# A four-layer spectral network with a dilation behind it: a new order of fc1 and fc2 steps in the mixing, and loads moved away from the rows of layers 1 and 3

## The chip, the cores and the metric

The kernel runs on one core of one Trainium2 chip. The metric is the device time of a run in microseconds, and the median over several runs is quoted. One execution was recorded by the hardware profiler; the profile describes that execution alone, and its span is the time from its first to its last instruction.

## What is computed

Eight images of 8 channels and 256 x 256 pixels, fp32 throughout. Cut to what matters:

```python
h = _gconv1x1(concat(groupnorm(x), grid), fc0_w, fc0_b)      # 4 groups, 10 channels each
for i in range(4):
    h1 = _spectral_conv(h, sp_w1[i], sp_w2[i])               # rfft2, 24 x 12 modes mixed, irfft2
    h2 = _gconv1x1(h, w_w[i], w_b[i])
    h = h1 + h2
    if i < 3:
        h = _gswish(h, betas[i])
h = _gswish(_gconv1x1(h, fc1_w, fc1_b), betas[3])            # 10 -> 128 channels in each group
x = x + _gconv1x1(h, fc2_w, fc2_b)                           # 128 -> 2 channels in each group
x = x + dilate3x3(groupnorm(x))                              # maximum over 3 x 3, border -2
```

The Fourier transforms are matrix products with tables of sines and cosines, since only 24 x 12 modes are kept.

## The kernel before

The images run one after another. For image b the kernel goes through four layers, and among their instructions it deals the steps of the "head" (fc1, swish and fc2) of the image before, so that the head's products on TensorE and its Silu on ScalarE fill the time around the layers' VectorE work. A third strand, the "tail" (the dilation), follows the head. Image 0 has no head or tail beside it; the head of image 7 runs alone after the last layer.

The order is written out by hand. Inside the block under a manual schedule the engines TensorE, VectorE, ScalarE and SP (the queue that issues most DMAs) run their instructions in the order in which the Python code emits them. The layers are generators; at each `yield` they hand out a string of letters, and the main loop emits one step for each letter (function `step`, lines 839 to 853):

- `f` first emits the additions to y that are due (`sum_up`), then one fc1 step. `F` is the same without `sum_up`.
- `c` emits one fc2 step and right after it the addition that this step makes due. `C` is the same, with the addition left for a later `f` or `c`.
- `t` emits one step of the tail.

One fc1 step (`first`, line 743) takes 512 pixels: four products on TensorE (line 753), one for each group, into four PSUM banks, and two Silu instructions on ScalarE, one for the first bank (line 754, 512 elements a partition) and one for the other three (line 755, 1536). The result lies in one of four buffers of the tile `act`. One fc2 step (`second`, line 758) uses up two such buffers: eight products (line 770) sum into one bank, and VectorE adds this bank to the tile y (line 777 for the first addition into a y tile, 779 for the others). A head has 128 fc1 and 64 fc2 steps.

PSUM is divided into two tags. `one` is a single bank, with 2 buffers; `tri` is three banks, with 2 buffers. An fc1 step takes one of each, an fc2 step one `one`, and the layers' own products take from the same two tags. A step whose buffer is still to be read by another engine waits for that engine.

The states that fc1 reads lie in DRAM (`stored`, written in layer 3 of the image at line 560). `load_state` (line 724) brings them back into SBUF in pieces of 256 KB (tile `hs`, 4 buffers, line 729), each nine fc1 steps before it is read. `load_y` (line 731) brings 256 KB of the input for the final addition (line 740). Both are issued from SP at the place where the step that calls them is emitted.

Within a layer after layer 0 the stages are:

1. `spectrum_h`: transposes on VectorE (line 359) and products for the Fourier transform over rows (`p_b`, lines 368 and 379). It hands out six `f` and three `c`.
2. `mix` (line 389): twelve VectorE instructions, six products (line 398) and six sums (line 401) in turn, then six short ones and 64 small products on TensorE (`p_f`, line 429, "the fold" below). Its yields in the layers 1 to 3 are the place of the first edit. `n` counts the twelve instructions.
3. `rows_of` (line 449): products that lay the mixed modes out over rows (`p_g`). In layers 0 and 2 these are 10 large products (line 462). In layers 1 and 3 they are 160 small ones (line 468: 32 x 32 weights, 66 columns). VectorE copies the results into `zt` (line 208).
4. `layer`: for each of the 11 chunks of the image the inverse transform and the 1 x 1 convolution (`burst`, `p_z`), and, in layers 0 to 2, the next forward transform.

In layer 3 a generator named `side` (`start` of the next image) is moved on beside the rows and the bursts: twice in the rows and twice in each chunk. It starts with the three loads of mixing weights for layer 0 of the next image (`load_sw`, 400 KB each, line 387), then normalises the next image in 20 steps (`spectrum_x`) and mixes layer 0 of it (`mix` with l == 0, where the weights are read). The weights of the layers 1 to 3 are loaded at the end of the layer before. The two loads of the next image itself (`load_x`, 1 MB each) are issued in the mixing of layer 3, at n == 2. The lines that the first edit touches:

```python
            if l == 0:
                if n % 2 or n > 7:
                    yield
            elif n not in (0, 2, 6, 10):
                yield "CF" if n in (1, 4, 7, 9) else "f"
...
        yield "fc"
```

Of the kernel before, what the change touches and what calls it, by code (L numbers as in the profile page):

```python
# [38 lines left out]
PIX = 2 * HW  # L39
# [6 lines left out]
def fno_dilate_kernel(ctx: ExitStack, tc: tile.TileContext, a: dict, out: bass.AP):  # L46
# [338 lines left out]
    def load_sw(l, k):  # L385
        t = sb.tile([128, G, 2 * WID, WID], F32, tag="sw", bufs=3)
        nc.sync.dma_start(t.rearrange("p g m i -> p (g m i)"), a["spw"][l, k])
        return t

    def mix(b, l, out_):  # L390

        s = [sb.tile([128, 3, 2, WID, G], F32, tag=f"S{i}", bufs=1, name=f"S{i}_{b}_{l}") for i in range(2)]
        bt, sw = out_["bt"], out_["sw"]
        for n in range(12):
            k, k2 = n // 4, n // 2 % 2
            pr = turned[:, 2, 1024 * k2 : 1024 * k2 + 800].rearrange("p (g m i) -> p g m i", g=G, i=WID)
            if n % 2 == 0:
                nc.vector.tensor_tensor(  # L398
                    pr, sw[k], bt[:, k2, k].unsqueeze(2).to_broadcast([128, G, 2 * WID, WID]), ALU.mult)
            else:  # L400
                nc.vector.tensor_reduce(  # L401
                    s[k2][:, k].rearrange("p s o g -> p (s o) g"),
                    pr.rearrange("p g m i -> p m g i"), AX.X, ALU.add,
                )
            if l == 0:
                if n % 2 or n > 7:
                    yield
            elif n not in (0, 2, 6, 10):
                yield "CF" if n in (1, 4, 7, 9) else "f"
            if n == 2 and l == 3 and b + 1 < n_img:  # L410
                load_x(b + 1)
        for i, (x, y, op) in enumerate((
                (s[0][:, :, 0], s[1][:, :, 1], ALU.subtract), (s[0][:, :, 1], s[1][:, :, 0], ALU.add),
                (s[1][:, :, 1], s[0][:, :, 0], ALU.subtract))):
            three = [t[:, :, :9].rearrange("p k (r o) g -> p k r (o g)", r=3) for t in (x, y)]
            nc.vector.tensor_tensor(fs[:, 0:3, i].rearrange("p r k o g -> p k r (o g)"), *three, op)
            nc.vector.tensor_tensor(fs[:, 3, i, :, 0], x[:, :, 9], y[:, :, 9], op)
        yield "fc"

        n_f = 6 * NO * G  # L420
        if l > 0:
            nc.vector.tensor_copy(fz[:, :, :, 24], cz[:, l])
        if l < 2:
            nc.vector.tensor_copy(fz[:, :, :, 25], cz[:, 4 if l == 0 else 3])
        one, tri, banks = ps_four(f"p_f_{b}_{l}")
        for term in range(2):
            for r in range(4):
                for q in range(4):
                    mm(banks[q][part(r), :n_f], fold[part(q), term, :],
                       fs[part(q), r, term : term + 2].rearrange("p t k o g -> p (t k o g)"),  # L430
                       start=term == 0, stop=term == 1)
        if l == 0:
            mr = out_["mr"]
            nc.vector.tensor_tensor(dc[:, 0:1], mr[:, 0:1], mr[:, 1:2], ALU.mult)
            out_["wcn"] = sb.tile([128, 32], F32, tag="wcn", bufs=1, name=f"wcn_{b}")
            nc.vector.tensor_scalar(out_["wcn"], wc, mr[:, 1:2], None, ALU.mult)
            for r in range(4):
                mm(one[part(r), n_f : n_f + NO * G], dc, wm[:, NO * r : NO * (r + 1), :], start=True, stop=True)
        cols = fz.rearrange("p o g c -> p (o g) c")
        nc.vector.tensor_copy(  # L440
            cols[:, :, 6:24].rearrange("p x (q c) -> p q c x", q=3),
            tri[:, :, :n_f].rearrange("p q (c x) -> p q c x", c=6))
        nc.vector.tensor_copy(
            cols[:, :, 0:6].rearrange("p x c -> p c x"), one[:, :n_f].rearrange("p (c x) -> p c x", c=6))
        if l == 0:
            nc.vector.tensor_tensor(
                fz[:, :, :, 24], one[:, n_f : n_f + NO * G].rearrange("p (o g) -> p o g", o=NO), cz[:, 0], ALU.add)

    def rows_of(b, l, side):

        zv = zt[:, :, :, : NBLK * WID].rearrange("p r f (n o) -> p o n r f", n=NBLK)
        yield "ffc"
        for oi in range(NO):
            name = f"p_g_{b}_{l}_{oi}"
            if oi == 0:
                one, tri, banks = ps_four(name)
            else:
                tri = ps_tri(name)
                banks = [tri[:, r, :] for r in range(3)]
            if l % 2 == 0:  # L460
                for r, p in enumerate(banks):
                    mm(p[:, : NBLK * CS * NQ], fz[part(r), oi].rearrange("p g k -> p (g k)"),
                       rowg[part(r)].rearrange("p n j r -> p (n j r)"), start=True, stop=True)
            else:
                for g in range(G):
                    for j in range(NQ):
                        for r, p in enumerate(banks):
                            mm(p[part(j), NBLK * CS * g : NBLK * CS * (g + 1)], fz[part(r), oi, g, :],  # L468
                               rowg[part(r), :, j, :], start=True, stop=True)
            n = NBLK * CS * NQ  # L470
            for i, r in enumerate((1, 2, 3, 0) if oi == 0 else (0, 1, 2)):
                src = banks[r][:, :n]
                if l % 2 == 0:
                    dst = zv[:, NO * r + oi].rearrange("p n r f -> p n f r")
                    src = src.rearrange("p (n f r) -> p n f r", n=NBLK, r=CS)
                else:
                    dst = zv[:, NO * r + oi].rearrange("p n r f -> p f n r")
                    src = src.rearrange("p (f n r) -> p f n r", f=NQ, n=NBLK)
                copy(i, dst, src)
            yield "fcf"[oi]  # L480
            if l == 3 and oi != 1:
                next(side, None)
        if l < 3:
            yield "t"

# [3 lines left out]
            for g in range(G):  # L489
                nc.sync.dma_start(h[32 * g : 32 * g + 6, c].rearrange("p f w -> p (f w)"), a["xp"][b, c, g])  # L490

    def layer(b, l, out_, stored, side):
        group_in_f = l % 2 == 1

        def turn(c, halves=(0, 1)):
# [70 lines left out]
        if l == 3:  # L566
            for c in range(NCH):
                burst(c)
                yield "fct" if c < 8 else "fc"
                next(side, None)  # L570
                if c + 1 < NCH:
                    yield "f"
                next(side, None)
                if c in ((3, 4, 5) if alone[0] else (6, 8, 9)):
                    yield "ready"
                if c > 3 and not alone[0]:
                    read_x(b + 1, c - 4)
            return
# [49 lines left out]

    def start(b, out_):
        if b < n_img:  # L630
            out_["sw"] = [load_sw(0, k) for k in range(3)]
            yield from spectrum_x(b, out_)
            yield from mix(b, 0, out_)

# [8 lines left out]
        for i in range(c, NCH):  # L643
            read_x(b + 1, i)

    def layers(b, stored, d, then):

        for l in range(4):
            if l > 0:
                yield from spectrum_h(b, l, d)
                yield from mix(b, l, d)
            yield from rows_of(b, l, then)
            yield from layer(b, l, d, stored, then)
        yield "stored"
        yield from rest(b, then)

# [47 lines left out]
        yield  # L707


    sums_due = []  # L710

    def sum_up():

        while sums_due:
            sums_due.pop(0)()

    def head(b, stored, stats):
# [6 lines left out]
        def load_state(k):  # L724

            if k < NQ * NCH:
                j, c = k // NCH, k % NCH
                hs[k] = sb.tile([128, PIX], F32, tag="hs", bufs=4, name=f"hs_{b}_{k}")
                nc.sync.dma_start(hs[k], stored[c][:, PIX * j : PIX * (j + 1)])

        def load_y(t):

            if t < 8:
                if last:
                    y = ya[:, 1 + 2 * t : 3 + 2 * t, 1 : HW + 1]
                else:
                    y = sb.tile([128, 512], F32, tag="yp", name=f"y_{b}_{t}")
                    y = y.rearrange("p (s w) -> p s w", s=2)
                box[t] = y
                nc.sync.dma_start(  # L740
                    y, a["x"][b].rearrange("c (p t s w) -> (c p) t s w", p=16, t=8, s=2)[:, t])

        def first():

# [94 lines left out]
    def step(kind):  # L839

        for i, (b, (done, first, second, _)) in enumerate(heads):
            if kind in "fF" and done[0] < STEPS:
                if kind == "f":
                    sum_up()
                return first()
            if kind in "cC" and 2 * done[1] < STEPS:
                second()
# [12 lines left out]
    with tc.manual_schedule(engines={PE, DVE, ACT, SP}):  # L860
# [2 lines left out]
            pass  # L863
        for b in range(n_img):
            stored = [dram.tile([128, NQ * PIX], F32, tag=f"hs{c}", name=f"stored_{b}_{c}") for c in range(NCH)]
            ahead, new, n_ready = {}, None, 0
            for n in layers(b, stored, d, start(b + 1, ahead)):
                if n == "ready":
                    if new is None:
                        if b + 1 < n_img:  # L870
# [9 lines left out]
                else:  # L880
                    for kind in n or "":
                        if kind == "t":
                            tail()
                        elif heads:
                            step(kind)
            d = ahead
        while heads:
            for kind in "ffc":
                if heads:
# [168 lines left out]
```

## Time and profile before

| | us |
|---|---|
| median of 3 runs | 3826.1 (3812.43 to 3826.25) |
| profiled execution, its own time | 3819.83 |
| its span | 3818.0 |
| mean granted TensorE clock, share of full speed | 0.975 |
| ScalarE, Silu of three banks (L755), 1024 times | 1493.3 busy, 1458 ns each |
| ScalarE, Silu of one bank (L754), 1024 times | 616.3 busy, 602 ns each |
| fc1 products (L753) | 1150.2 busy |
| fc2 products (L770) | 1024.3 busy |

The profile names an instruction by engine, line and tiles (`p_fc<-hs,c_w` is a product of the state and a constant into the tile p_fc). PE is TensorE, PEld its loads of weights, DVE VectorE, ACT ScalarE, POOL GpSimd and SP the queue of SyncE. Every fp32 product appears as two instructions, so an fc1 step is 8 products and an fc2 step 16. In the timeline a line gives the start and the length of one instruction or of a run of like ones, and in brackets the idle time of the engine before it with what ended it. Matmuls are pipelined and their ends are modelled; starts are the safer thing to read.

### The profile page before, as it was taken

The numbers are of one execution on the slowest core, as the hardware profiler recorded it, in microseconds if no ns is written. First come the engines' busy times: TensorE is split into PE (matmuls) and PEld (weight loads), VectorE is DVE, ScalarE is ACT, GpSimd is POOL, SyncE is SP. The second block draws the span as 40 slices with busy tenths as digits, with TensorE's granted clock in tenths as the row PEclk, the third lists the DMA queues.
The fourth block names the chain that finished last, engine by engine and source line by source line (L and its number), as shares of the span: only waits on it lengthen the run. The fifth ranks groups of instructions, "written<-read, shape, count | busy, mean of one in ns | idle before, by whom it ended". The sixth has DMA issues, their size and how long they took to land.

```text
span 3818.0 us, 117724 instructions
## 1 busy us (share of the span) xinstructions
PE 3567.4 (93%) x53432; PEld 1299.9 (34%) x53432; DVE 2422.9 (63%) x3781; ACT 2821.9 (74%) x2919; POOL 117.1 (3%) x202
## 2 busy tenths in 40 slices
PE   5768999999999999999999999999999999999997
PEld 2323333333333333333333333333333333333222
DVE  6776665557775667756776577765777566772443
ACT  2435777777777777787777877777777777778986
POOL 1000000000000000000000000000000000000000
PEclk7878999999999999999999999999999999999998
DMA  3005111432225212362123512144222532225221
GB/s 87 15 31 191 49 45 47 147 113 62 73 84 174 82 57 70 99 193 61 49 67 111 185 56 66 53 150 138 59 73 66 174 91 67 67 67 178 79 86 49
DMA packets 114067, 344.91 MB, mean 90 GB/s; under 512 B 15984, under 2 KB 18480, under 8 KB 98144
## 3 DMA queue, kind: packets, MB, share of 16 engines
q1 hardware_dynamic: 95392, 276.32, 24.0%
q0 software_dynamic: 18176, 61.07, 5.0%
q8 instruction: 420, 6.88, 0.8%
q14 instruction: 79, 0.65, 0.1%
HBM read 213.33 MB, written 123.74 MB: 88 GB/s over the span
## 4 chain that ended last, share of the span: by engine, by line
PE 74%; DVE 14%; ACT 5%; issue 4%; DMA 2%; POOL 0%; ACTq 0%; DVEq 0%; POOLq 0%
PE p_fc L770 21%; PE p_fc L753 20%; PE p_z L551 9%; PE p_z L548 7%; PE p_d L516 7%; PE p_z L545 3%; DVE turned L499 3%; PE p_u L530 3%; DVE S L401 2%; ACT act L755 2%; DVE turned L398 2%; DVE y L779 2%; PE p_g L468 2%; DMA yin<-y_rows 2%; ACT act L754 1%
## 5 line engine op out<-in xcount | busy, mean ns | idle before, releaser
L755 ACT ACTIVATE act<-p_fc 128x1536 f32<-128x1536 f32 x1024 | 1493.3, 1458 | 0.0
L753 PE MATMUL p_fc<-hs,c_w 32*128 32x512 f32 x8192 | 1150.2, 626 | 50.1 <-ACT act L754 19.1
L770 PE MATMUL p_fc<-act,c_w 128*32 128x512 f32 x8192 | 1024.3, 602 | 8.2 <-DVE y L779 6.3
L754 ACT ACTIVATE act<-p_fc 128x512 f32<-128x512 f32 x1024 | 616.3, 602 | 417.7 <-PE p_fc L753 408.4
L499 DVE STREAM_TRANSPOSE turned<-h 128x1024 f32<-128x1024 f32 x528 | 632.3, 1225 | 183.0 <-ACT h L556 182.4
L556 ACT ACTIVATE h<-p_z 128x512 f32<-128x512 f32 (+1 forms) x528 | 512.0, 1021 | 226.5 <-PE p_z L551 226.5
L779 DVE TENSOR_TENSOR y<-p_fc,y 128x512 f32<-128x512 f32 x392 | 267.6, 683 | 589.1 <-PE p_fc L770 586.4
L753 PEld LDWEIGHTS p_fc<-hs,c_w 32*128 32x128 f32 x8192 | 363.3, 184 | 638.9 <-ACT act L754 269.8
L770 PEld LDWEIGHTS p_fc<-act,c_w 128*32 128x32 f32 x8192 | 226.5, 109 | 709.8 <-issue 323.1
L551 PE MATMUL p_z<-c_binv,zt 32*128 32x256 f32 x5632 | 411.7, 406 | 0.0
L548 PE MATMUL p_z<-h,c_wt 32*32 32x512 f32 x8448 | 374.3, 607 | 8.4 <-ACT act L754 4.2
L551 PEld LDWEIGHTS p_z<-c_binv,zt 32*128 32x128 f32 x5632 | 259.6, 187 | 311.6 <-issue 298.4
L516 PE MATMUL p_d<-turned,c_fw 32*32 32x480 f32 (+1 forms) x9216 | 308.3, 540 | 0.7 <-DVE turned L499 0.4
L520 ACT ACTIVATE turned<-p_d 128x1440 f32<-128x1440 f32 x144 | 183.1, 1271 | 90.2 <-PE p_d L516 87.0
L558 ACT ACTIVATE h<-p_z,c_bias 128x512 f32<-128x512 f32 (+1 forms) x176 | 186.6, 1111 | 77.9 <-PE p_z L551 77.8
L208 DVE COPY zt<-p_g 128x264 f32<-128x264 f32 x304 | 155.4, 610 | 70.3 <-PE p_g L468 52.7
L401 DVE TENSOR_REDUCE S<-turned 128x80 f32<-128x800 f32 x192 | 188.9, 984 | 5.9
L398 DVE TENSOR_TENSOR turned<-t,B 128x800 f32<-128x800 f32 x192 | 188.7, 983 | 0.9
L516 PEld LDWEIGHTS p_d<-turned,c_fw 32*32 32x32 f32 x9216 | 127.2, 103 | 165.9 <-issue 65.0
L359 DVE STREAM_TRANSPOSE turned<-zt 128x960 f32<-128x960 f32 x96 | 176.7, 1865 | 2.5
L548 PEld LDWEIGHTS p_z<-h,c_wt 32*32 32x32 f32 x8448 | 94.3, 103 | 188.8 <-DVE y L779 54.1
L530 PE MATMUL p_u<-turned,c_stack 128*32 128x480 f32 (+1 forms) x1152 | 136.7, 543 | 11.5 <-DVE turned L519 6.2
(186 smaller groups left out, 1704.2 us busy)
## 6 DMA issues: line engine op xcount, KB each, us to landing
stored<-h SPq DMA_DIRECT2D x88, 1024.0 KB
hs<-stored SPq DMA_DIRECT2D x352, 256.0 KB
t<-in_spw SPq DMA_DIRECT2D x96, 400.0 KB
yin<-y_rows POOLq DMA_DIRECT2D x56, 512.0 KB, 5.3
h<-in_xp SPq DMA_DIRECT2D x352, 48.0 KB
turned<-in_xw SPq DMA_DIRECT2D x16, 1024.0 KB
y<-in_x SPq DMA_DIRECT2D x56, 256.0 KB
y_rows<-y POOLq DMA_DIRECT2D x56, 256.0 KB, 2.5
```

The costliest lines, as they stand in the source:

```text
L398: nc.vector.tensor_tensor(pr, sw[k], bt[:, k2, k].unsqueeze(2).to_broadcast([128, G, 2 * WID, WID]), ALU.mult)
L401: nc.vector.tensor_reduce(s[k2][:, k].rearrange("p s o g -> p (s o) g"), pr.rearrange("p g m i -> p m g i"), AX.X, ALU.add,)
L499: nc.vector.transpose(dst[:, 2 * i : 2 * i + 2], h[:, c, 2 * i : 2 * i + 2].rearrange("p f (s x) -> p f s x", s=2))
L516: mm(banks[q][part(v % 4), : 240 * n], fw8[part(q), v, :], t[part(q), :, :, v, : NBLK * WID], start=v < 4, stop=v >= 4)
L548: mm(o, wt[part(q), l, g, :], h[part(q), c, f, :], start=True, stop=False)
L551: mm(banks[q][:, HW * s : HW * (s + 1)], zt[part(q), 2 * c + s].rearrange("p f o -> p (f o)"), binv[part(q), :], start=False, stop=s == 1)
L556: nc.scalar.activation(dst, src, AF.Silu)
L753: mm(banks[g], w1[part(g), blk, :], hs[k][part(g), :], start=True, stop=True)
L754: nc.scalar.activation(act[:, 0, :], one, AF.Silu)
L755: nc.scalar.activation(act[:, 1:4, :], tri, AF.Silu)
L770: mm(acc[part(g), :], w2[:, g, 15 - rb - i : 47 - rb - i], act[:, g, :], start=i == 0, stop=i == 1)
L779: nc.vector.tensor_tensor(y, sums, y, ALU.add)
```

## The change

There are four edits.

1. In the mixing of layers 1 to 3 the step of n == 1 hands out "fc" in the place of "CF", and those of n == 4, 7 and 9 hand out "fC". The letter `F` is gone, and `step` no longer knows it.
2. `hold(True)` at the start of `rows_of` in layers 1 and 3 (with `hold(False)` in effect in the others) makes `load_state` and `load_y` put their DMA issues on a list; `hold(False)` at the end of the rows issues what is on the list. The tiles are still allotted where they were.
3. The three loads of mixing weights for the next image's layer 0 move from the start of `side` (in the rows of layer 3) to the chunks 1, 2 and 3 of layer 3, one in each, behind that chunk's write of the state on SP. For image 0 they stay at the start of the kernel.
4. The dictionary that receives them is handed through `layers` and `layer` for this.

```diff
             elif n not in (0, 2, 6, 10):
-                yield "CF" if n in (1, 4, 7, 9) else "f"
+                yield {1: "fc", 4: "fC", 7: "fC", 9: "fC"}.get(n, "f")
...
     def rows_of(b, l, side):

         zv = zt[:, :, :, : NBLK * WID].rearrange("p r f (n o) -> p o n r f", n=NBLK)
+        hold(l % 2 == 1)
         yield "ffc"
...
             if l == 3 and oi != 1:
                 next(side, None)
+        hold(False)
         if l < 3:
             yield "t"
...
                 if c in ((3, 4, 5) if alone[0] else (6, 8, 9)):
                     yield "ready"
+                if 0 < c < 4 and b + 1 < n_img:
+                    ahead.setdefault("sw", []).append(load_sw(0, c - 1))
                 if c > 3 and not alone[0]:
                     read_x(b + 1, c - 4)
...
         if b < n_img:
-            out_["sw"] = [load_sw(0, k) for k in range(3)]
+            if b == 0:
+                out_["sw"] = [load_sw(0, k) for k in range(3)]
             yield from spectrum_x(b, out_)
             yield from mix(b, 0, out_)
...
+    held = [None]
+
+    def now_or_later(f):
+
+        if held[0] is None:
+            f()
+        else:
+            held[0].append(f)
+
+    def hold(on):
+
+        due, held[0] = held[0], [] if on else None
+        for f in due or ():
+            f()
...
-                nc.sync.dma_start(hs[k], stored[c][:, PIX * j : PIX * (j + 1)])
+                now_or_later(lambda: nc.sync.dma_start(hs[k], stored[c][:, PIX * j : PIX * (j + 1)]))
...
-                nc.sync.dma_start(
-                    y, a["x"][b].rearrange("c (p t s w) -> (c p) t s w", p=16, t=8, s=2)[:, t])
+                now_or_later(lambda: nc.sync.dma_start(
+                    y, a["x"][b].rearrange("c (p t s w) -> (c p) t s w", p=16, t=8, s=2)[:, t]))
...
-            if kind in "fF" and done[0] < STEPS:
-                if kind == "f":
-                    sum_up()
+            if kind == "f" and done[0] < STEPS:
+                sum_up()
                 return first()
```

## The prediction

> **What bounds the kernel now.** I read the page first, then the groups of TensorE, then the timeline of one mixing stage, then the sums by stretch for all mixing stages and all odd rows, last the waits around line 468. From the page:
>
> ```profile
> span 3818.0 us, 117724 instructions
> PE 3567.4 (93%) x53432; PEld 1299.9 (34%) x53432; DVE 2422.9 (63%) x3781; ACT 2821.9 (74%) x2919; POOL 117.1 (3%) x202
> PE 74%; DVE 14%; ACT 5%; issue 4%; DMA 2%; POOL 0%; ACTq 0%; DVEq 0%; POOLq 0%
> ```
>
> TensorE is busy for 93% and holds 74% of the chain, yet the chain also runs over VectorE and ScalarE. So the question is where TensorE waits. In the mixing stage (lines 389 to 410) of image 3, layer 1, the timeline (start, us, engine, line) has:
>
> ```profile
> 1361.24 1.14 PE L753 MATMUL p_fc<-hs,c_w 32*128 32x512 f32 x8 [0.73 <-ACT act L754]
> 1361.94 0.68 DVE L779 TENSOR_TENSOR y<-p_fc,y 128x512 f32<-128x512 f32 x1
> 1362.68 1.92 PE L770 MATMUL p_fc<-act,c_w 128*32 128x512 f32 x16 [0.30 <-DVE y L779]
> 1364.54 2.02 PE L753 MATMUL p_fc<-hs,c_w 32*128 32x512 f32 x16
> 1365.69 0.60 ACT L754 ACTIVATE act<-p_fc 128x512 f32<-128x512 f32 x1 [1.33 <-PE p_fc L753]
> 1366.49 2.25 PE L770 MATMUL p_fc<-act,c_w 128*32 128x512 f32 x16
> 1367.52 0.61 ACT L754 ACTIVATE act<-p_fc 128x512 f32<-128x512 f32 x1
> 1368.67 2.01 PE L753 MATMUL p_fc<-hs,c_w 32*128 32x512 f32 x16
> 1370.62 2.27 PE L770 MATMUL p_fc<-act,c_w 128*32 128x512 f32 x16
> ```
>
> An fc2 step (L770, "c" below) starts at 1366.49 and the next at 1370.62: a round of one c and two fc1 steps (L753, "f") takes 4.13 us. A c alone holds TensorE 1.85 us (1362.68 to 1364.53), an f 0.88 (the second of two at 1364.54 starts at 1365.42), so a round has 1.85 + 2 x 0.88 = 3.61 us of work. The other 0.52 us is a loop: c, then f behind it, then ScalarE's read of that f's single bank, and only then the next c, which writes that bank. The slot is told by the times: the read L754 at 1365.69 ends at 1366.29, the c starts at 1366.49. The rounds of c at n = 4, 7, 9 all show it; the first shows the two gaps printed. The sums by stretch say that every such stage is alike (us; busy of PE, PEld, DVE, ACT, POOL; granted clock, DMA share, GB/s):
>
> ```profile
> 448.47:469.76 21.29, 20.05 (x152) 5.34 (x152) 15.83 (x24) 17.30 (x19) 0.55 (x1) 1.00 0.22 57
> 679.72:701.01 21.29, 20.04 (x153) 5.34 (x153) 15.83 (x24) 17.30 (x19) 0.54 (x1) 1.00 0.43 146
> ```
>
> 21.29 us in layer 1 at 57 GB/s and in layer 3 at 146: transfers do not matter in it. There are 21 of these (images 1 to 7, layers 1 to 3). The second place is the rows of layers 1 and 3 (line 468, 160 small products each):
>
> ```profile
> L468 PE MATMUL p_g<-c_rowg,fz 32*32 32x66 f32 x5120 | 70.9, 238 | 34.2 <-issue 23.4 <-DVE zt L208 8.9 <-DVE fz L443 1.6
> 1383.60:1393.20 9.60, 6.94 (x352) 4.20 (x348) 4.96 (x9) 3.09 (x3) 0.00 (x0) 1.00 0.21 58
> 1617.50:1629.00 11.50, 9.87 (x352) 4.85 (x348) 7.07 (x13) 3.12 (x3) 0.00 (x0) 0.70 0.11 28
> 1842.50:1850.10 7.60, 6.97 (x352) 4.30 (x351) 4.99 (x10) 3.10 (x3) 0.00 (x0) 1.00 0.27 73
> ```
>
> Equal work takes 7.6 to 11.5 us, and the idle time is "issue": neither data nor a semaphore was late.
>
> **What the Trainium skill says.** "Runtime: NRT & Kernel Launch", Instruction fetch mechanics: instructions are fetched in blocks of 16 KiB (256 instructions) over a DMA queue of the sequencer's own, and crossing a block is mostly hidden. The page's queue q8 (420 packets, 6.88 MB: 16 KB each; 106864 TensorE instructions / 256 = 417) is that stream. In these rows it is not hidden: 128 loads and 128 products pass in 1.5 us, and the stalls of about 2 us (1390.4, 2304.3) end about 2.3 us after their block's packet starts, though the packet takes 0.93. "DMA: Bandwidth & Descriptors", Issuing engines are not separate DMA queues: all queues share 16 engines, so loads can slow a fetch; packets of q8 take 0.88 to 1.6 us here. "TensorE: Matmul & The Clock Gate", What's actually happening: idle TensorE drops to half clock; 0.70 in the stretch at 1617.5 agrees. "PSUM — Partial Sum Buffer", Specifications: 8 banks of 512 fp32. The tiles "one" (2 x 1) and "tri" (2 x 3) fill all, so no f or c gets a spare bank.
>
> **The change part by part.**
>
> (1) Deal in the mixing, lines 408-409. The counts stay 9 f and 5 c; the order c f f | c f f | c f f | c f f | f c becomes f c f | f c f | f c f | f c f | f c... with adds (L779) as before except the first, now right behind its c. No step is added. Before a c the number of f's ahead goes from 3 to 4 acts, which the 4 act buffers just hold, and the last "fc" of the stage already had 4; a c then reads only acts finished long ago (before, its later weight loads waited for ACT L755, which makes 2.25 of 1.92).
>
> I carry the rows above through the new order, each step starting at the latest of: TensorE free (0.88 after an f, 1.85 after a c); its bank free (ScalarE's L754 starts 1.16 us after an f, or 1.83 after the previous f's, lasts 0.60, and 0.20 later TensorE may write; an add ends 2.68 after its c). Banks are taken in the order in which they come free. Clock 13xx: f1 57.52, c1 58.39, f2 60.24, f3 61.12, c2 62.20 (ScalarE's read of f2), f4 64.05, f5 65.55 (add of c2), c3 66.42, f6 68.27, f7 69.15, c4 70.22, f8 72.07, f9 72.95 (its triple bank until 73.24), c5 74.10, and the fold (L429) 75.95. It was at 1378.88, so 2.93 us are saved. The same rules on the old order give its measured starts (59.37, 61.3, 62.68), so I trust them to some 0.3 us. What is late next: ScalarE, 1.83 per f or 3.66 per round, against TensorE's 3.61. Bounds: TensorE's bare sum is 9 x 0.88 + 5 x 1.85 = 17.17 from 57.52, at most 4.19 saved; if f1 takes the bank that L382 frees at 58.12 and f5 one that costs 0.45, 2.0 is saved. I take 2.93: 21 x 2.93 = 61.5 us, range 42 to 88. VectorE (15.8 of 21.3 us) has cover: after the change its two products and sums per round plus the add come to 2.67 x 0.98 + 0.69 = 3.3 us.
>
> (2) Held loads. In rows of layers 1 and 3 the loads of hs (L729, 256 KB) and y (L740) leave SP after the rows instead of in them: one or two hs each, 14 rows. Same number, later by up to 9 us. A state is loaded 9 f's ahead: of the three loads after 1611.08 (1622.47, 1641.75, 1648.49) the third marks its first reader, 37 us later; held to 1629, 19 us remain. A 256 KB transfer takes 2.5 us (y_rows in the page), so nothing waits; SP has no other work in the rows. Were that cover gone, each late us costs up to 14. The queue's next entries, stored and h, come later.
>
> (3) Mixing weights for the next image, 3 x 400 KB. They leave SP at 1611.45 to 1612.44 now, just before the rows; after, behind the stored writes of chunks 1 to 3 of layer 3. First reader: mix of layer 0, 20 steps of the side generator on, at chunk 9, some 40 us after chunk 3. Chunks 1 to 3 carry 400 KB more per 6.6 us, 60 GB/s on the layer's 209; I take 1.5 us in all for slower dilation loads there (0 to 7: six images by about 1 us).
>
> What (2) and (3) bring to the rows: idle time over the 14 rows is 20.8 us beside the 0.63 us wait for zt; layer 3 takes 10.04 us in the mean, layer 1, with less traffic, 8.82. All of this difference gone is 7 x 1.22 = 8.5 us. But the stalls of layer 1 are as long where a block border falls badly (9.6 and 7.6 at like traffic), so contention is the smaller part: a fetch packet slows by 0.1 to 0.5 us. I take 0.35 x 14 = 5 us; from 0 to 9, and about 8 us either way if block borders shift or a half-clock stretch comes or goes (1617.5: 0.70 for 11.5 us, about 3 us).
>
> Sum on the profiled execution (span 3818.0, its own time 3819.83): 3819.8 - 61.5 - 5 + 1.5 = 3754.8. The median of the three runs, 3826.1, lies 6.3 above it; on that base 3761. I say 3760.
>
> **Rivals.**
> (a) TensorE's bare sum: ScalarE never falls behind, 4.19 a stage, rows fully mended: 3826 - 88 - 9 = 3729. For: VectorE and ScalarE each fit into it; against: ScalarE's 3.66 per round. 0.10.
> (b) Only the first gaps go: banks fall less well, 1.0 a stage, 21 us, and nothing in the rows: 3805. For: a bank's choice decides 0.5 us at a time, and the trace has one odd choice, at 1361.24, where f takes the bank of the f before. Against: the loop c-f-ScalarE-c is cut by the order alone. 0.13.
> (c) Slower: c is given the bank of the f just in front of it. Then it waits for that f's read, 1.96 after it instead of 0.88, in each of 5 rounds: a round is 1.96 + 1.85 + 0.88 = 4.69 against 4.13, 0.56 x 5 x 21 = 59 us, less 5: 3880. It decides from the point where more than half of the c's take that bank. Against: the bank of the f before comes free earlier. 0.08.
> (d) It does not reach the end: the 3 us saved are waited out in the rows for ScalarE. For: f9's read ends 1.05 us after the fold starts (0.69 before). Against: that is 0.36 us, and TensorE is the bound behind it. 3820. 0.04.
>
> **How the numbers follow.** The forecast has 0.65, with 3735 to 3795 its own range (2.0 to 4.0 a stage, rows -10 to +9). (a), (b) and it are faster by over 0.5% (19 us, about what this measurement can tell from none): 0.88. (d) is the same: 0.04. (c) 0.08. The range 3732 to 3800 leaves out (c), (d) and parts of (a) and (b).
>
> **What would show it.** Mixing stages of 18.4 us (17.2 to 19.4), rounds of c of 3.7, no wait of L753 for L754 of 0.73 at their start, L770 at 1.92 throughout; odd rows of 9.0 us in the mean with "issue" still there; no wait for hs. Wrong it is if stages keep 21 us, or if c's wait for L754 right after their f.

## The result, and the profile after

| | before | after |
|---|---|---|
| median of 4 runs, us | 3823.33 (3812.43 to 3826.25) | 3765.4 (3764.59 to 3771.87) |
| ratio, with its 95% interval | | 0.9857 (0.9834 to 0.9881) |
| span of the profiled execution | 3818.0 | 3763.8 |

The change makes the kernel 58 us faster by the medians; the two profiled executions differ by 54.2 us. From the page of the changed kernel:

```profile
span 3763.8 us, 117725 instructions
PE 3536.7 (94%) x53432; PEld 1288.3 (34%) x53432; DVE 2423.2 (64%) x3781; ACT 2824.3 (75%) x2919; POOL 117.3 (3%) x202
PE 72%; DVE 16%; issue 5%; ACT 4%; DMA 2%; POOL 0%; ACTq 0%; DVEq 0%; POOLq 0%
```

The instruction counts of all engines are as before, so what has gone is waiting. Of the 54 us, 31 stand in TensorE's busy time (3567.4 us before), since a step that stops in its middle counts as busy. Line numbers have moved: fc1 is L773 now, its Silus L774 and L775, fc2 L790, its additions L797 and L799, the small products of the rows L469. The sums by stretch of two mixing stages (layers 1 and 3 of image 1), with the columns as before:

```profile
447.63:466.73 19.10, 18.60 (x159) 4.83 (x162) 15.82 (x24) 17.36 (x19) 0.55 (x1) 1.00 0.23 63
673.90:693.00 19.10, 18.60 (x156) 4.82 (x156) 15.82 (x24) 17.36 (x19) 0.54 (x1) 1.00 0.45 162
```

All 21 stages have gone from 21.29 to 19.10 us, with the same work on VectorE (15.8) and ScalarE (17.4). The timeline of the same stage that was shown of before (image 3, layer 1):

```profile
1342.59 1.92 PE L790 MATMUL p_fc<-act,c_w 128*32 128x512 f32 x16
1344.44 1.14 PE L773 MATMUL p_fc<-hs,c_w 32*128 32x512 f32 x8
1345.21 0.68 DVE L799 TENSOR_TENSOR y<-p_fc,y 128x512 f32<-128x512 f32 x1
1345.60 0.60 ACT L774 ACTIVATE act<-p_fc 128x512 f32<-128x512 f32 x1
1345.95 1.14 PE L773 MATMUL p_fc<-hs,c_w 32*128 32x512 f32 x8 [0.37 <-DVE y L799]
1347.02 1.93 PE L790 MATMUL p_fc<-act,c_w 128*32 128x512 f32 x16
1348.88 2.02 PE L773 MATMUL p_fc<-hs,c_w 32*128 32x512 f32 x16
1350.83 1.92 PE L790 MATMUL p_fc<-act,c_w 128*32 128x512 f32 x16
```

The round from the c at 1347.02 to the one at 1350.83 takes 3.81 us where it took 4.13. One new wait is printed: the f at 1345.95 waits for an addition that VectorE begins only at 1345.21, because a sum of the mixing stands in front of it. The group of the small products, over the whole run:

```profile
L469 PE MATMUL p_g<-c_rowg,fz 32*32 32x66 f32 x5120 | 68.7, 236 | 23.5 <-issue 11.8 <-DVE zt L208 9.5 <-DVE fz L443 1.6
```

"issue" has fallen from 23.4 to 11.8 us, and the wait for zt has not changed. Summed over all stages, measured from first product to first product, the two spans differ like this:

| stage | before, us | after, us | difference |
|---|---|---|---|
| mixing of layers 1 to 3, images 1 to 7 (with the end of the Fourier step) | 530.7 | 484.6 | -46.1 |
| rows of layer 1, images 1 to 7 | 70.3 | 68.4 | -2.0 |
| rows of layer 3, images 1 to 7 | 77.3 | 67.2 | -10.1 |
| rows of layers 1 and 3, image 0 | 15.1 | 12.4 | -2.6 |
| all else | 3124.6 | 3131.2 | +6.6 |

### The profile page after: what moved, and what is told of

It reads as the page before. It is cut to its first block, busy times and chain, and to the rows that moved or that the text cites. A ratio compares the mean times of both kernels' runs of the same rounds, so it can differ in the third digit from the quotient of the medians.

```text
span 3763.8 us, 117725 instructions
## 1 busy us (share of the span) xinstructions
PE 3536.7 (94%) x53432; PEld 1288.3 (34%) x53432; DVE 2423.2 (64%) x3781; ACT 2824.3 (75%) x2919; POOL 117.3 (3%) x202
## 4 chain that ended last, share of the span: by engine, by line
PE 72%; DVE 16%; issue 5%; ACT 4%; DMA 2%; POOL 0%; ACTq 0%; DVEq 0%; POOLq 0%
PE p_fc L790 19%; PE p_fc L773 18%; PE p_z L553 9%; PE p_z L550 7%; PE p_d L518 7%; PE p_z L547 3%; DVE y L799 3%; DVE turned L501 3%; PE p_u L532 3%; DVE S L401 3%; DVE turned L398 2%; DMA yin<-y_rows 2%; PE p_g L469 2%; DVE turned L359 1%; PE p_b L368 1%
## 5 line engine op out<-in xcount | busy, mean ns | idle before, releaser
L775 ACT ACTIVATE act<-p_fc 128x1536 f32<-128x1536 f32 x1024 | 1492.2, 1457 | 0.3 <-PE p_fc L773 0.3
L773 PE MATMUL p_fc<-hs,c_w 32*128 32x512 f32 x8192 | 1137.7, 627 | 43.2 <-DVE y L799 20.8
L790 PE MATMUL p_fc<-act,c_w 128*32 128x512 f32 x8192 | 1011.7, 602 | 1.8 <-issue 1.7
L774 ACT ACTIVATE act<-p_fc 128x512 f32<-128x512 f32 x1024 | 615.6, 601 | 361.9 <-PE p_fc L773 350.6
L799 DVE TENSOR_TENSOR y<-p_fc,y 128x512 f32<-128x512 f32 x392 | 267.8, 683 | 536.7 <-PE p_fc L790 536.7
L773 PEld LDWEIGHTS p_fc<-hs,c_w 32*128 32x128 f32 x8192 | 356.9, 183 | 615.8 <-ACT act L774 252.6
L790 PEld LDWEIGHTS p_fc<-act,c_w 128*32 128x32 f32 x8192 | 222.1, 109 | 702.8 <-issue 322.1
L560 ACT ACTIVATE h<-p_z,c_bias 128x512 f32<-128x512 f32 (+1 forms) x176 | 186.7, 1111 | 77.3 <-PE p_z L553 77.1
```

The costliest lines, as they stand in the source:

```text
L773: mm(banks[g], w1[part(g), blk, :], hs[k][part(g), :], start=True, stop=True)
L774: nc.scalar.activation(act[:, 0, :], one, AF.Silu)
L775: nc.scalar.activation(act[:, 1:4, :], tri, AF.Silu)
L790: mm(acc[part(g), :], w2[:, g, 15 - rb - i : 47 - rb - i], act[:, g, :], start=i == 0, stop=i == 1)
L799: nc.vector.tensor_tensor(y, sums, y, ALU.add)
```

## Experiments

Eleven runs follow, the last of them the changed kernel again. In every one I read the time, the length of the 21 mixing stages (equal to 0.02 us within a run, but for one stage in each of the two kernels with spread rows) and the mean length of the odd rows of images 1 to 7, from the first to the last small product: 8.82 us in layer 1 and 10.04 in layer 3 before, 8.61 and 8.45 after.

**The order alone.** Edit 1 on the kernel before:

```diff
-                yield "CF" if n in (1, 4, 7, 9) else "f"
+                yield {1: "fc", 4: "fC", 7: "fC", 9: "fC"}.get(n, "f")
```

> Edit 1 alone on the kernel before. If the mixing stage is worth what the two traces show (21.29 to 19.10 us, 21 stages), this run is 46 us faster than before, about 3777, with mixing stages of 19.1 us and odd rows as before (mean 9.4 us). Rival: part of the gain in the rows comes from the order too (the rows start with other buffers free); then the odd rows fall below 9 us here as well and the run is 52 us or more faster.

Measured: 3775.47 against 3824.89 us, ratio 0.9861 (0.9836 to 0.9887), 49 us, between the 46 expected and the 52 of the rival. Stages of 19.10; rows 8.70 and 9.76 us, 9.23 in the mean and not below 9. The order gives the stage and nothing that stands out in the rows; most of the 58 us is here.

**The loads alone.** Edits 2 to 4 on the kernel before, the order as it was.

> Edits 2 to 4 alone on the kernel before. If the loads slow the instruction fetch in the rows: mixing stages stay 21.29 us, the odd rows fall from 9.4 to about 8.5 us in the mean (layer 3 by 1.4 us, layer 1 by 0.3), and the run is 10 to 13 us faster, less up to 4 us in the chunks of layer 3. Rival: the shorter rows after the change are an accident of where the 256-instruction borders fall; then the rows here are as before within 0.3 us in the mean and the time is the same.

Measured: 3814.07 us, 0.9974 (0.9962 to 0.9986), 11 us faster. Stages 21.29 to 21.30; rows of layer 3 8.40, of layer 1 8.73. What stands out is in the rows of layer 3; layer 1 has moved no more than it does between two traces of the changed kernel (8.61 and 8.51). The two halves add up to 60 us; the whole gave 58, and its interval is 45 to 63.

**Which of the loads: states held alone, weights moved alone.** The first keeps the `hold` and `now_or_later` of the change and leaves the weights in the rows; the second takes `hold(l % 2 == 1)` and `hold(False)` out and keeps

```diff
+                if 0 < c < 4 and b + 1 < n_img:
+                    ahead.setdefault("sw", []).append(load_sw(0, c - 1))
```

> Edit 2 alone (states and y held, mixing weights loaded in the rows of layer 3 as before). If the 1.2 MB of weights is what disturbs the rows of layer 3: its rows stay within 0.5 us of 10.0 and those of layer 1 fall by 0.2 to 0.4, the run 2 to 5 us faster. Rival: the states and y matter as much; then the rows of layer 3 fall by 0.7 us or more and the run is 6 us faster or more.

> Edits 3 and 4 alone (mixing weights of the next image moved to chunks 1 to 3 of layer 3, states and y not held). If the weights' 1.2 MB is what disturbs the rows of layer 3, their mean falls from 10.0 to about 8.7 us here too and the chunks of layer 3 lose up to 0.7 us an image; 4 to 8 us faster. Rival: holding the states is what clears the rows; then the rows of layer 3 stay above 9.5 us and the time is the same within 3 us.

Measured: held alone 3818.86 us, 0.9985 (0.9975 to 0.9995), 6 us faster, rows of layer 3 8.62 and of layer 1 9.41 (one of them 13.09, with half clock in it; the other six 8.79). Weights moved alone 3815.61 us, 0.9973 (0.9958 to 0.9988), 11 us faster (4 to 8 expected), rows of layer 3 8.76 and of layer 1 8.89. Either edit clears the rows of layer 3 by itself. The rival of the first had its numbers, but the reason that it gives, the traffic of states and y, is not it. The SP queue shows why. Its issues around the rows of image 3, layer 3, in the kernel before (these rows run from 1617.5 to 1629.0):

```profile
1611.08 0.32 SPq L729 DMA_DIRECT2D hs<-stored  x1
1611.45 1.37 SPq L387 DMA_DIRECT2D t<-in_spw  x3
...
1622.47 0.33 SPq L729 DMA_DIRECT2D hs<-stored  x1
```

In the changed kernel (rows from 1590.9 to 1598.7):

```profile
1584.46 0.32 SPq L749 DMA_DIRECT2D hs<-stored  x1
1593.50 0.32 SPq L749 DMA_DIRECT2D hs<-stored  x1
```

And with the states held alone (rows from 1623.2 to 1631.7):

```profile
1610.78 1.40 SPq L387 DMA_DIRECT2D t<-in_spw  x3
1616.79 0.33 SPq L746 DMA_DIRECT2D hs<-stored  x1
1625.86 0.33 SPq L746 DMA_DIRECT2D hs<-stored  x1
```

The loads of states are not held at all. They leave 6.4 us before the rows and 2.7 us into them, in the changed kernel as in that with the hold alone; before, they left 6.4 us ahead and 5.0 into rows that were longer. What an SP load waits for is its buffer, which comes free when fc1 has read the state in it: each of the loads shown leaves 0.05 to 0.09 us after the last product of an fc1 step. SP has nothing else to do meanwhile, so a load that the code puts behind the rows still leaves at that moment. What the hold does change is the order on SP: before, the three loads of weights stood behind the load at 1611.08 and came out with it, 6 us before the rows; with the hold they stand in front of it and leave at 1610.78, 12.4 us before the rows (1623.2). Before, packets of 1.5 MB start in the six us ahead of these rows; with the hold it is 0.3 MB. Moving the weights away reaches the same end.

So nearly all of the weights pass ahead of the rows. What they do there the fetch packets of the trace tell (queue q8). The last packet that starts before the rows of layer 3, in us from their start, in the images where the borders of the blocks fall alike (to within 24 instructions of 256):

| | images 1, 3 and 5 | image 7 |
|---|---|---|
| before | -0.4, -0.2, -0.6 | -3.5 |
| order alone | -0.6, -0.7, -0.5 | -3.7 |
| states held alone | -3.7, -3.6, -3.6 | -3.0 |
| weights moved alone | -3.6, -3.4, -3.7 | -3.7 |
| after | -3.7, -3.5, -3.5 | -3.7 |

With the weights in front of them these packets start some 3 us later; they take 0.91 to 1.02 us then and are no shorter without. Image 7 has no next image and so no such weights: in the kernel before, its rows take 8.64 us where those of images 1, 3 and 5 take 10.2, 11.5 (with half clock in it) and 9.7.

**What stalls the rows.** 32 small products more at the start of the kernel, half a block of instructions; nothing else moves:

```diff
+    for _ in range(32):
+        mm(p[0:6, 2, :32], fc0x[part(0), :], wt[part(0), 0, 0, :], start=True, stop=True)
```

> Kernel before with 32 more small products (128 TensorE instructions, half a block of 256) at its very start; nothing else moves. If the stalls in the odd rows are set by where the borders of the instruction blocks fall, the rows of layer 1 change places: images 3, 5 and 7 (9.6 to 9.9 us) become short and images 2, 4 and 6 (7.6 to 8.1) long, with about the same sum. Rival: they are set by the loads that happen to run; then each image keeps its length within 0.4 us.

One run: 3820.51 us, the same as before. Sums by stretch of the rows of layer 1 in images 1 to 4:

```profile
479.30:486.70 7.40, 6.77 (x352) 4.35 (x348) 4.96 (x9) 3.11 (x3) 0.00 (x0) 1.00 0.27 76
929.50:939.30 9.80, 7.17 (x352) 4.34 (x348) 4.98 (x9) 3.15 (x3) 0.00 (x0) 0.96 0.21 57
1387.10:1395.10 8.00, 6.93 (x350) 4.21 (x347) 4.97 (x9) 3.15 (x3) 0.00 (x0) 1.00 0.26 70
1840.50:1850.00 9.50, 7.12 (x352) 4.29 (x348) 5.00 (x10) 3.09 (x3) 0.00 (x0) 0.99 0.21 59
```

Before, images 1 to 7 had 9.0, 7.7, 9.6, 7.6, 9.9, 8.1 and 9.8 us; with the shift 7.4, 9.8, 8.0, 9.5, 7.5, 10.0 and 7.5. Long and short have changed places in all seven, at a sum of 59.7 against 61.8. The length of a row in layer 1 is set by where a block border falls in it. In layer 3 the shift alone takes the mean from 10.04 to 9.28 us, with the loads where they were; so there the border counts beside the weights.

The traces show the border itself. Counting TensorE's records (products and loads of weights) from the start of the run, all 226 stalls of over 0.25 us that are put down to "issue" among the small products, in the 13 traces, come behind the 193rd or 194th record of a group of 256, in the shifted kernel too.

**More traffic.** 2 MB more, DRAM to DRAM, issued from SP at the start of each odd row of images 1 to 7:

```diff
+        if l % 2 and b > 0:
+            for i in range(2):
+                t = dram.tile([128, 2048], F32, tag="more", bufs=2, name=f"more_{b}_{l}_{i}")
+                nc.sync.dma_start(t, a["xw"][b, :, i])
```

> Kernel before with 2 MB more of transfers (DRAM to DRAM, read by nobody) issued from SP at the start of each odd row of images 1 to 7. If transfers slow the instruction fetch: fetch packets in these rows take well over 1.1 us in the mean, and the rows of layer 1 grow by 1 us or more each. Rival: the fetch does not feel other traffic; then the rows of layer 1 keep their mean of 8.8 us within 0.4.

One run: 3862.39 us, rows of 12.19 and 12.30 us in the mean. The whole run's group:

```profile
L472 PE MATMUL p_g<-c_rowg,fz 32*32 32x66 f32 x5120 | 76.4, 254 | 54.6 <-issue 45.6 <-DVE zt L208 7.1 <-DVE fz L443 1.6
```

The rows do feel traffic: "issue" has doubled. The other half of the expectation failed. The fetch packet before each of the 26 stalls still takes 0.88 to 1.3 us (one 1.98), and TensorE still goes on 2.2 to 2.7 us after the packet starts (one 3.2); yet the stalls last up to 4.4 us. So the packet is not slower, it starts later: in six of the 26 stalls 0.3 to 2.1 us after TensorE has run dry, where in the kernel before it always started at least 0.26 us ahead of that. There, 19 stalls of over 0.25 us in these rows ended 2.2 to 2.9 us after the start of a fetch packet, and they came to 18.7 us; after, 11 stalls with the same delay came to 10.0 us.

**Why the order helps.** The kernel before with one f more at n == 1 and one fewer at the end:

```diff
-                yield "CF" if n in (1, 4, 7, 9) else "f"
+                yield {1: "fCF", 4: "CF", 7: "CF", 9: "CF"}.get(n, "f")
...
-        yield "fc"
+        yield "c" if l > 0 else "fc"
```

> Kernel before, with one fc1 step more handed out at n == 1 (fCF) and one fewer at the end of the mixing (c for fc). TensorE's order of steps is then that of the changed kernel; the places of the steps and additions among VectorE's twelve instructions stay as before. If the gain comes from a fc2 step that reads acts one step older (4 ahead in place of 3), no fc2 step takes 2.18 us to the next fc1 step any more, and the stage is 18.9 to 19.7 us, 33 to 50 us faster in all. Rival: the gain comes from where the additions stand on VectorE; then the stage stays above 20.5 us and the run is less than 17 us faster.

Measured: 3793.66 us, 0.9908 (0.9889 to 0.9927), 31 us (33 to 50 expected); stages of 19.83 us, 0.13 outside the expected band. No c takes more than 1.93 us there. One f moved from the end of the stage to its front, with the additions where they were, gives 1.46 of the 2.19 us. By the starts of the weight loads, all 21 stages of a kernel are alike. What a step takes beyond 0.88 us (f behind f), 1.07 (c behind f) and 1.85 (any step behind a c), in us a stage:

| | before | this variant | after |
|---|---|---|---|
| second f and second c, at the start | 1.36 | 1.36 | 0 |
| c's that stop in their middle | 0.68 | 0 | 0 |
| third of three f's, at the end | 1.33 | none | none |
| other waits | 0.05 | 0.38 | 1.02 |

One more c behind an f, for one f less behind an f, adds 0.19 to both new orders. So the older acts are worth 0.68 us. More comes from the end of the stage, which was c f f f c: the third f in a row waited for ScalarE to read a three-bank buffer, the longest single wait of the stage.

```profile
1372.81 2.93 PE L753 MATMUL p_fc<-hs,c_w 32*128 32x512 f32 x18
1374.47 1.44 ACT L755 ACTIVATE act<-p_fc 128x1536 f32<-128x1536 f32 x1
1375.96 0.31 PEld L753 LDWEIGHTS p_fc<-hs,c_w 32*128 32x128 f32 x6 [1.05 <-ACT act L755]
```

No run separates the older acts from the shorter row of f's; that both waits are gone is read from the traces. The places of the additions on VectorE give the other 0.73. The wait at the start is as long in this variant as before, with another cause: the f of n == 3 waits for an addition that stands behind two mixing instructions.

```profile
1352.64 0.68 DVE L779 TENSOR_TENSOR y<-p_fc,y 128x512 f32<-128x512 f32 x1
1353.37 1.14 PE L753 MATMUL p_fc<-hs,c_w 32*128 32x512 f32 x8 [1.10 <-DVE y L779]
```

The changed kernel issues that addition at n == 1, right behind its c, and has no such wait there; its other waits, 0.63 us at the f of n == 7 and 0.39 at that of the end, are for later additions.

**Two tries for more.** First, on the changed kernel, the addition of n == 4 at once and the last f one instruction earlier:

```diff
-            elif n not in (0, 2, 6, 10):
-                yield {1: "fc", 4: "fC", 7: "fC", 9: "fC"}.get(n, "f")
+            elif n not in (0, 2, 6, 11):
+                yield {1: "fc", 4: "fc", 7: "fC", 9: "fC"}.get(n, "f")
```

> Changed kernel with the addition of n == 4 right behind its fc2 step (fc for fC) and the step of n == 11 handed out at n == 10. The two waits left in its mixing stage, for the additions at n == 5 (0.6 us) and n == 11 (0.4 us), should go: stages of 18.1 to 18.5 us in place of 19.10, 13 to 20 us faster than the changed kernel. Rival: VectorE, made to wait for fc2 earlier, comes late for its own sums and the fold waits for it; then the stage is 19.1 us or more.

Measured: 3761.06 us, 0.9827 (0.9808 to 0.9847), stages of 18.66 us, short of the 18.1 to 18.5 expected. Between the fold and the rows 0.19 us of that is given back, so 0.25 us a stage remain, which would be 5 us in all, where 13 to 20 were expected. By the times it can't be told from the changed kernel, whose interval it overlaps.

Second, the six steps of an odd row in the same order, but inside the runs of small products:

```diff
-        yield "ffc"
+        yield "ff" if l % 2 else "ffc"
...
                 for g in range(G):
+                    if g == 2:
+                        yield "ccf"[oi]
...
-            yield "fcf"[oi]
+            yield ("f", None, None)[oi] if l % 2 else "fcf"[oi]
```

> Changed kernel; in the odd rows the same fc1 and fc2 steps in the same order, but placed inside the runs of small products (fc2 after 2 of 4 groups of the first two runs, fc1 inside the third) and not between them. If a stall is the part of a block's fetch (2.2 to 2.9 us) that the work already queued behind the border doesn't cover, more of it is covered: idle time put down to issue in the odd rows of images 1 to 7 falls from 10.0 us to below 6, the rows from 8.5 us in the mean to about 8.1, and the run is 3 to 6 us faster than the changed kernel. Rival: the steps inside the runs wait for PSUM banks that the rows hold, and the rows grow; then the mean is 8.8 us or more.

> e8_early and e9_spread together. If both gains stand apart: stages of 18.66 us, rows as in e9_spread, some 8 to 12 us faster than the changed kernel, about 3755. Rival: the gain of 0.25 us a stage is eaten in the rows, where ScalarE is further behind; then it is as e9_spread within 2 us.

> The changed kernel once more, on the same chip and in the same rounds as e9_spread and e10_both, so that these compare with it; about 3765, stages of 19.10 us.

Run in turn with these two, the changed kernel had 3775.84 us (0.9859, 0.9833 to 0.9885), the spread rows 3804.79 (0.9945, 0.9924 to 0.9967) and both tries together 3803.4 (0.9937, 0.9918 to 0.9955). The spread is slower, as its rival said, though for the wait the other way round:

```profile
L471 PE MATMUL p_g<-c_rowg,fz 32*32 32x66 f32 x5120 | 78.3, 237 | 37.3 <-issue 14.0 <-ACT act L777 13.3 <-DVE zt L208 8.2
```

With only two f's and no c ahead of it, the first run of small products waits for ScalarE to read the three-bank buffer of the f before (13.3 us over the run): the rows wait for a bank that a step holds. "issue" in the odd rows of images 1 to 7 is 9.5 us, in 6 longer stalls in place of 11, so the fetch was not covered better either. From fold to layer the odd stages grew by 1.9 us (layer 1) and 1.6 (layer 3). Both tries together are within 2 us of the spread alone, as the rival of that run has it; where the shorter stage (18.66 us there too) was lost is not shown.

## Why the prediction was right, step by step

The forecast of 3760 stands against 3765.4. The sum on the profiled executions was -65 us, the measured one -54.2. That the forecast came so near is in part luck: the mixing gave 15 us less than its term and the rows 7 more, and the median before fell by 3 with its fourth run. The forecast's terms were right in direction, and two of them stand on a wrong reason.

- **The mixing, -61.5 predicted, -46 measured.** The term was mis-sized: 2.93 us a stage, measured 2.19. Its rule that a step may start 0.88 us after an f is true of an f behind an f only. By the weight loads, from which the 0.88 was read, a c follows an f after 1.07 us at the earliest, in 463 pairs before and 484 after, and 1.07 is usual in these stages. In the carried clock this adds 0.20 at c1 and 0.20 at c3. A further 0.30 comes from f8 to c5: the addition of c4 stands behind the last sum on VectorE and begins at 1353.16, 2.33 us after its c and not 1.99. The three, with a few hundredths of rounding, are the 0.74 by which the fold came late: 19.17 us after f1, where 18.43 was predicted.
- **The loop that was to be cut.** I read the 0.52 us a round as a c waiting for ScalarE's read of the bank of an f. That failed: f to c takes 1.07 us after the change too, so 0.19 of it is the step itself and stays (the c at 1347.02 comes 1.07 behind its f, though ScalarE's last read of a single bank had ended at 1346.20). The other 0.33 was inside the c. Its later weight loads, before and after:

```profile
1367.38 0.11 PEld L770 LDWEIGHTS p_fc<-act,c_w 128*32 128x32 f32 x1 [0.32 <-issue]
1367.68 0.15 PEld L770 LDWEIGHTS p_fc<-act,c_w 128*32 128x32 f32 x6 [0.20 <-ACT act L755]
```

```profile
1347.48 0.13 PEld L790 LDWEIGHTS p_fc<-act,c_w 128*32 128x32 f32 x4 [0.30 <-issue]
1347.91 0.13 PEld L790 LDWEIGHTS p_fc<-act,c_w 128*32 128x32 f32 x4 [0.30 <-issue]
```

  Before, the c at 1366.49 broke off until ScalarE had finished an act (L755); after, it reads one that is a step older. I had named this wait, as a by-product. With it went the wait of the third f, 1.33 us, which the forecast names nowhere; it is in its sum only because the start of the fold was measured before and carried after. TensorE's order is a periodic c f f both ways but for the end, so the new order is one fc1 step more in hand and no three f's in a row.
- **The start of the stage.** The 0.73 us in front of the second f and the 0.30 in front of the second c went, as predicted. ScalarE did not become the bound; the place of the additions on VectorE did: 0.63 us at the f of n == 7, which the forecast had, and 0.39 at that of the end, which it had not.
- **The held loads, "leave SP after the rows instead of in them".** That failed, as the SP queue above shows: they leave when their buffer comes free. Nothing waited for them, as predicted, but because nothing was delayed.
- **The rows, -5 predicted (0 to -9), -12.1 measured in images 1 to 7.** I gave 0.35 us to each of 14 rows. Layer 1 gained 0.28 a row, layer 3 1.45. The mean difference between the two layers, which I had as the upper bound and did not believe, is gone with the weights. But a fetch packet was not slowed by 0.1 to 0.5 us, as I had it: it started some 3 us later. The page that I named for it speaks of DMAs that engines issue; that the fetch gives way to them is what the weights and the added traffic show. That a badly placed border costs as much as traffic, in layer 1, is confirmed by the shift.
- **Weights in the chunks of layer 3, +1.5.** Not told apart: the stretch from there to the next image is 4.5 us longer after the change, but also 3.4 longer with the shift, which moves no load, and 0.4 with the changed kernel run again.
- **Rivals.** The bare sum of TensorE (a) counted the same 0.88; with 0.19 more for each of five c's the floor from the first f to the fold is 17.17 + 0.95 = 18.1 us, and the best try had 18.73. Banks that fall badly (b, c) did not show: apart from the waits named, no step in the stage waits for a bank. The gain was not waited out in the rows (d): from fold to rows it is 4.70 us both ways.

The +6.6 us under "all else" is not traced to the change: in the repeat of the changed kernel the same sum is 2.1 us under that of before. Part of it may be the clock. Outside the start and the end, the record has 30.7 us at half clock in both profiled executions, at other places; in the repeat 6.8 us, and there the span was 3753.5 us. That the stretch at 1617.5 agrees with a drop of idle TensorE to half clock, as I had it, holds in part. The half clock there begins at 1620.7, after 3.4 us in which the longest gap was 1.33; and three of the six such pieces of the kernel before (at 822, 1733 and 2191 us) begin after 3.4 us without a gap. Idle time alone does not explain them.

## What to carry to other kernels

Where a consumer on one engine stops in its middle, look at the age of what it reads, and where several producers stand in a row, count their buffers: here one step handed out earlier mended both. A load on SP left when its own wait was met and the queue in front of it was empty, not where the code stands; to keep it out of a stretch, read in the trace what it waits for, and what stands in front of it. Count the instructions of a stage of small products: here a border between two blocks cost up to 2 us, and it cost more where other transfers ran when the next block was to be fetched.

## What the runs showed of the hardware

- By the starts of their weight loads, an fc2 step (128 rows by 32 columns) follows an fc1 step (32 by 128) after 1.07 us at the earliest, where a second fc1 step mostly follows after 0.85 to 0.88. From an fc2 step to an fc1 step the shortest is 1.85 us, in which its 16 products are issued.
- Stalls on instruction fetch stand at one place in every 256 instructions of TensorE. After a stall TensorE goes on 2.2 to 2.9 us behind the start of the packet of its next 256 instructions, though the packet takes about 1 us. The Trainium skill, "Runtime: NRT & Kernel Launch", Instruction fetch mechanics, calls the crossing mostly hidden; in these rows it cost up to 2.0 us, and with 2 MB of other traffic up to 4.4.
- Other transfers delayed the start of a fetch packet and not the packet: by some 3 us with 1.2 MB of weights ahead of it.
- Half clock comes and goes in pieces of 3.4 us or multiples of it: 92 us of it with the added traffic, 51 with the spread rows, 7 to 41 in the other traces.
